# A selective-scan kernel: a quarter of the second half's products made a chunk ahead, norm and gate passes of the last direction in other places

## The chip, the cores and the metric

The kernel runs on one core of a Trainium2 chip. Its time is the device time of one execution in microseconds (us). The kernel before was run three times: 32539.59, 32542.47 and 32545.17 us, median 32542.47. The engines are PE (matmul; its weight loads are listed apart as PEld), DVE (vector), ACT (activation functions), POOL (general), and SP, which issues most of the DMAs. Each engine works through its own instructions in the order in which they were written, and semaphores tie the engines to one another.

## What is computed

The input is an image of 256 x 256 tokens with 128 channels. Layer 0 is a gated attention along the rows, layer 1 a selective scan in four directions; each is added to its input. The change lies in layer 1. Cut to what matters there:

```python
xz = x @ w_in.T;  xi, z = jnp.split(xz, 2, axis=-1);  z = silu(z)
xc = silu(depthwise_conv3x3(xi) + conv_b)              # 256 channels
xs = four orders of the tokens: rows, columns, and both backwards
dts, Bs, Cs = split(x_proj_w @ xs)                     # 8 + 16 + 16 rows
delta = softplus(dt_w @ dts + dt_bias)
# for each direction, channel and each of 16 states n, along the tokens t:
#   h[t] = exp(delta[t] * A[n]) * h[t-1] + (delta[t] * x[t]) * B[n, t]
#   y[t] = sum over n of h[t] * C[n, t]  + D * x[t]
y = sum of the four directions, each put back into row order
y = (y - mean) / sqrt(var + 1e-5) * ln_w + ln_b        # over the channels
out = x + (y * z) @ w_out.T
```

## The kernel before

**Stages.** The group norm, the attention and the convolution come first and take about 5.7 ms. The scan takes the rest; the change is in it alone.

**Directions and chunks.** The directions are worked one after the other, in the order 2, 1, 3, 0 (`ORDER`), each in 128 chunks of 512 tokens. The first three write their sum so far to DRAM (`store`); the next one loads it (`load_sum`, tile `yl`) and adds it on PE. The last direction (`finish`) adds all, normalizes over the channels, multiplies with the gate z, and projects to the output.

**Steps.** A chunk has eight steps, `g` = 0 to 7, called the first to the eighth step here. A step works on 32 channels with all 16 states on 128 partitions: four groups of 32 partitions, and for each group four states, one after the other along the free axis. So a step has four places, `n` = 0 to 3, each with one `exp` on ACT (`dA`, or `dAl` at n = 0; L1081) and one scan on DVE (L1107). Three of the four inputs of the scans are made by DVE in one multiplication for the next step (`times_B`, L838, which reads `ur`, spread over the partitions by PE). The fourth input, that of n = 0, is made by another way: ACT multiplies the transposed delta*x (`duT`) with the transposed B (`B_t`), 16 products of 128 x 128 for each half of the channels (`products`, tile `bt0` for steps one to four, `bt1` for steps five to eight, one buffer each; L797), and PE turns them back step by step (`turn_back`, tile `bl`, L809). After a step POOL saves the last column of h (L1126) and multiplies h with C (L1127). PE sums over the states for four steps together (`sums`, L853): for the steps five to eight at the second step of the next chunk, for the steps one to four at the end of the sixth and the start of the seventh.

**Work in pieces.** Everything that prepares the next chunks is written as generators, and at each place, between the exp and the scan, the loop takes a piece from each: one of `turning` (duT for the next chunk), one of every generator in `later` (`store`, `finish`), one of `preparing` (`prepare`, for the chunk after the next), and `counts[g][n]` pieces of `multiplying`, each of them one product on ACT. The order of the instructions on each engine follows from that by hand; there is no planner.

- `prepare(q + 2)` begins at n = 1 of the sixth step of chunk q and goes on into chunk q + 1. Its pieces that matter here: `pb` on PE at n = 0 of the eighth step, `bc` on ACT, which reads it, at n = 2 of the eighth (L710), `pv` on PE at n = 3, abs and relu at n = 1 and 2 of the first step of the next chunk, then exp, log(1+...) and so on, and `lg`, the Ln, at n = 0 of the third step (L758). [...] a table load stands before the Ln and another before the next exp.
- `products(q + 1, 0)` is put in line at n = 2 of the sixth step and has to be done when `turn_back` for the next chunk is written, at n = 3 of the eighth. `products(q, 1)` is put in line at n = 1 of the second step and has to be done at n = 3 of the fourth.
- `finish` begins at n = 0 of the fourth step of the next chunk. `until(a, b)` lets b - a places pass. Its 17th piece, at n = 0 of the eighth step, is the first of four `yn` passes (L952), which subtract the mean and divide; PE turns `yn` at n = 3 of the second step a chunk later, and the two `gz` passes (L971) scale with ln_w and ln_b. POOL then multiplies with z.
- PSUM tiles with the tag "mm" (`pb`, `pv`, `tpb`, `tpz`, `ysum`, `po` and others) share two buffers; the exps use three PSUM buffers (`dA`) and two in SBUF (`dAl`); `bx` has eight.

Of the kernel before, what the change touches and what calls it, by code (L numbers as in the profile page):

```python
# [66 lines left out]
def attention_and_scan_kernel(  # L67
# [611 lines left out]
    def until(now, then):  # L679

        for _ in range(then - now):
            yield
# [121 lines left out]
    def turn_back(q, g):  # L804

        bl = sps.tile([P, T], F32, name="bl", bufs=1)
        bt = products_of[q, g // 4]
        for b in range(4):
            nc.tensor.transpose(  # L809
                bl[:, b * P : (b + 1) * P], bt[:, b, g % 4].rearrange("t j c -> t (j c)"), ident  # L810
            )
        return bl
# [97 lines left out]
    def finish(q, yos):  # L910

        a = steps[q][1]
        yl = summed.pop(q)
        yield
        sums_ = []
        for g in range(2):
            ps = sps.tile([P, 2, DI], F32, name="ysum", tag="mm")
            add_sum(  # L920
                ps,
                yl[:, 2 * g : 2 * g + 2, :],
                [
                    (ps[:, j, h * P : (h + 1) * P], yos[h][:, (2 * g + j) * P : (2 * g + j + 1) * P])
                    for j in range(2)
                    for h in range(2)
                ],
            )
            sums_.append(ps)
            yield  # L930
        yield
        ys = io.tile([P, 4, DI], F32, name="ys", tag="yt", bufs=1)
        for g, ps in enumerate(sums_):
            nc.scalar.copy(ys[:, 2 * g : 2 * g + 2, :], ps)
            yield
        zt = io.tile([P, 2, T], F32, name="zl", bufs=1)
        nc.sync.dma_start(zt, z_d[:, a : a + T].rearrange("(h p) t -> p h t", p=P))
        st = io.tile([P, 4, 6], F32, name="yst")
        mv = io.tile([P, 4, 2], F32, name="ymv")
        rs = io.tile([P, 4], F32, name="yrs")  # L940
        nb = io.tile([P, 4], F32, name="ynb")
        for j in range(4):
            nc.vector.bn_stats(st[:, j, :], ys[:, j, :])
        for j in range(4):
            nc.vector.bn_aggr(mv[:, j, :], st[:, j, :])
        rsqrt(nc, rs, mv[:, :, 1], 1e-5, neg_half)
        nc.gpsimd.tensor_tensor(nb, mv[:, :, 0], rs, ALU.mult)
        nc.gpsimd.tensor_scalar(nb, nb, -1.0, None, ALU.mult)
        yield from until(6, 16)
        yn = io.tile([P, 4, DI], F32, name="yn", tag="yl", bufs=1)  # L950
        for j, now, then in ((0, 16, 19), (1, 19, 20), (2, 20, 23), (3, 23, 27)):
            nc.scalar.activation(  # L952
                yn[:, j, :],
                ys[:, j, :],
                AF.Identity,
                bias=nb[:, j : j + 1],
                scale=rs[:, j : j + 1],
            )
            yield from until(now, then)
        tps = []  # L960
        for h in range(2):
            tp = sps.tile([P, T], F32, name="tpz", tag="mm")
            for j in range(4):
                nc.tensor.transpose(
                    tp[:, j * P : (j + 1) * P], yn[:, j, h * P : (h + 1) * P], ident
                )
            tps.append(tp)
        yield from until(27, 30)
        gz = io.tile([P, 2, T], F32, name="gz", bufs=1)
        for h, tp in enumerate(tps):  # L970
            nc.scalar.activation(  # L971
                gz[:, h, :], tp, AF.Identity, bias=lnb_s[:, h : h + 1], scale=lnw_s[:, h : h + 1]
            )
            yield
        yield from until(32, 36)
        nc.gpsimd.tensor_tensor(gz, gz, zt, ALU.mult)
        yield from until(36, 40)
        xr = io.tile([P, 4, D], F32, name="xr", bufs=1)
        nc.sync.dma_start(xr, x2_d[a : a + T, :].rearrange("(j p) c -> p j c", p=P))
        yield from until(40, 55)  # L980
        po = sps.tile([P, 4, D], F32, name="po", tag="mm")
        nc.tensor.matmul(po, ident, xr, start=True, stop=True)
        for j in range(4):
            for h in range(2):
                nc.tensor.matmul(
                    po[:, j, :],
                    gz[:, h, j * P : (j + 1) * P],
                    wout_s[:, h, :],
                    start=False,
                    stop=True,  # L990
                    skip_group_check=True,
                )
        yield from until(55, 58)
        xo = io.tile([P, 4, D], F32, name="xo", tag="xr", bufs=1)
        nc.scalar.copy(xo, po)
        nc.sync.dma_start(out[a : a + T, :].rearrange("(j p) c -> p j c", p=P), xo)

    NQ = len(steps)
# [4 lines left out]
    def piece(*dues):  # L1003
        for due in dues:
            while due:
                try:
                    next(due[0])
                    return
                except StopIteration:
                    due.pop(0)  # L1010

    def drain(due):
        while due:
            piece(due)
# [42 lines left out]
    begin_sums(0, 0)  # L1057
    turning, multiplying, summing = [], [], []
    bls = {(0, 0): turn_back(0, 0)}

    counts = {1: [0, 2, 3, 3], 3: [2, 2, 2, 2], 5: [0, 0, 2, 2], 6: [1, 1, 2, 2], 7: [2, 2, 2, 0]}
    for s, (q, g) in enumerate(all_steps):
        k, a = steps[q]
        nxt = all_steps[s + 1] if s + 1 < len(all_steps) else None
        if g == 1:
            drs[q, 1] = spread_delta(q, 1)
        if g == 2 and q and steps[q - 1][0] != ORDER[0]:
            summed[q - 1] = load_sum(q - 1)
        if g == 2 and q + 2 < NQ:
            load(q + 2)  # L1070
        if g == 5 and q + 1 < NQ:
            drain(preparing)
            drs[q + 1, 0] = spread_delta(q + 1, 0)
        dr = drs[q, g // 4][:, g % 4, :]
        hs = bxs.pop((q, g))
        for n, i in enumerate((NB, *range(NB))):
            if i < NB:
                dA = sps.tile([P, T], F32, name="dA", bufs=3)
            else:
                dA = wk.tile([P, T], F32, name="dAl")  # L1080
            nc.scalar.activation(  # L1081
                dA, dr, AF.Exp, scale=A_s[:, k, g // 4, g % 4, i : i + 1]
            )
            if n == 0 and g == 3 and q:
                evacuate(q - 1, 1)
                begin_sums(q, 0)
            if n == 2 and g == 7:
                evacuate(q, 0)
                begin_sums(q, 1)
            if n == 0 and g == 1 and q:  # L1090
                drain([sums(q - 1, 1)])
            if n == 0 and g == 6:
                drain(summing)
            if g == 4 and n == 3 and q + 1 < NQ:
                turning.append(turn(q + 1))
            if g == 5 and n == 2 and q + 1 < NQ:
                multiplying.append(products(q + 1, 0))
            if g == 1 and n == 1:
                multiplying.append(products(q, 1))
            if g == 5 and n == 1 and q + 2 < NQ:  # L1100
                preparing.append(prepare(q + 2))
            piece(turning)
            pieces(later)
            piece(preparing)
            for _ in range(counts[g][n] if g in counts else 0):
                piece(multiplying)
            nc.vector.tensor_tensor_scan(  # L1107
                hs[:, i, :],
                dA,
                hs[:, i, :] if i < NB else bls.pop((q, g)),  # L1110
                0.0 if a == 0 else hst[:, g, i : i + 1],
                ALU.mult,
                ALU.add,
            )
            if n == 1 and nxt:
                bxs[nxt] = times_B(nxt[0], urs.pop(nxt))
            if n == 3 and nxt:
                bls[nxt] = turn_back(*nxt)
            if n == 3 and s + 2 < len(all_steps):
                urs[all_steps[s + 2]] = spread_du(*all_steps[s + 2])  # L1120
            if n == 3 and g == 5:
                summing.append(sums(q, 0))
                piece(summing)
        if g % 4 == 3:
            del drs[q, g // 4]
        nc.gpsimd.tensor_copy(hst[:, g, :], hs[:, :, T - 1])  # L1126
        nc.gpsimd.tensor_tensor(hs, hs, prepared[q][4], ALU.mult)  # L1127
        hcs[q, g] = hs
# [64 lines left out]
```

## Time and profile before

| | us | share of the span |
|---|---|---|
| median of three runs | 32542.47 | |
| profiled execution, its own time | 32538.74 | |
| its span, first to last instruction | 32537.0 | |
| PE busy | 24581.2 | 76% |
| DVE busy | 29634.3 | 91% |
| ACT busy | 25277.6 | 78% |
| POOL busy | 25719.5 | 79% |
| scans on DVE, n = 1 to 3 (L1107) | 15061.1 | x12192, 1262 ns each |
| times_B on DVE (L838) | 7067.5 | x4096, 1725 ns each |
| h * C on POOL (L1127) | 18604.5 | x4096, 4542 ns each |
| products on ACT (L797) | 5625.5 | x16384, 394 ns each |

The profile comes from one execution. Instructions on one engine can overlap by some tens of ns, so the spacing of their starts is shorter than their duration. In a timeline, a line gives the start in us from the first instruction, the duration, the engine, the line of the kernel, and in brackets how long the engine was idle before and what ended that. The clock that PE was granted is told as a share of its full speed.

### The profile page before, as it was taken

The numbers are of one execution on the slowest core, as the hardware profiler recorded it, in microseconds if no ns is written. First come the engines' busy times: TensorE is split into PE (matmuls) and PEld (weight loads), VectorE is DVE, ScalarE is ACT, GpSimd is POOL, SyncE is SP. The second block draws the span as 40 slices with busy tenths as digits, with TensorE's granted clock in tenths as the row PEclk, the third lists the DMA queues.
The fourth block names the chain that finished last, engine by engine and source line by source line (L and its number), as shares of the span: only waits on it lengthen the run. The fifth ranks groups of instructions, "written<-read, shape, count | busy, mean of one in ns | idle before, by whom it ended". The sixth has DMA issues, their size and how long they took to land.

```text
span 32537.0 us, 380541 instructions
## 1 busy us (share of the span) xinstructions
PE 24581.2 (76%) x122902; PEld 11561.7 (36%) x122902; DVE 29634.3 (91%) x28991; ACT 25277.6 (78%) x50438; POOL 25719.5 (79%) x11291
## 2 busy tenths in 40 slices
PE   5999989777777777777777777777777777777777
PEld 2555544223222223333333333333333333333333
DVE  7666643999999999999999999999999999999999
ACT  4555522888888888888888888888888888888887
POOL 3222200899999999999999999999999999999998
PEclk8999999777777777777777777777777777777777
DMA  3001023444444444444444444444444455554554
GB/s 137 29 28 30 28 93 123 110 108 109 110 109 108 108 109 119 118 118 119 120 120 118 117 119 121 119 119 118 120 120 118 118 123 123 122 121 121 122 122 112
DMA packets 2100469, 3518.55 MB, mean 108 GB/s; under 512 B 201112, under 2 KB 1187096, under 8 KB 2022560
## 3 DMA queue, kind: packets, MB, share of 16 engines
q1 hardware_dynamic: 2093296, 3476.09, 42.8%
q8 instruction: 967, 15.84, 0.2%
q10 hardware_dynamic: 5168, 18.12, 0.1%
q14 instruction: 1038, 8.50, 0.1%
HBM read 2754.18 MB, written 739.25 MB: 107 GB/s over the span
## 4 chain that ended last, share of the span: by engine, by line
DVE 31%; PE 27%; ACT 26%; issue 10%; POOL 5%; DMA 1%; DVEq 0%; SPq 0%; POOLq 0%; ACTq 0%
DVE bx L1107 17%; DVE bx L838 9%; PE yp L853 7%; ACT dA L1081 6%; PE ur L827 5%; ACT bt L797 4%; POOL bx L1127 2%; ACT dAl L1081 2%; PE pc L526 2%; ACT L758 2%; ACT L1081 2%; PE av L356 2%; POOL at L333 2%; ACT du L751 2%; PE atp L345 2%
## 5 line engine op out<-in xcount | busy, mean ns | idle before, releaser
L1127 POOL TENSOR_TENSOR bx<-bx,C_r 128x2048 f32<-128x2048 f32 x4096 | 18604.5, 4542 | 334.5 <-POOL hst L1126 6.0
L1107 DVE TENSOR_TENSOR_SCAN bx<-dA,hst,bx 128x512 f32<-128x512 f32 x12192 | 15061.1, 1262 | 455.3 <-ACT dA L1081 455.3
L1081 ACT ACTIVATE dA<-dr,A_s 128x512 f32<-128x512 f32 x12288 | 8345.5, 684 | 2974.6 <-DVE bx L1107 2865.2
L827 PE MATMUL ur<-du,spread 128*128 128x512 f32 x8192 | 5998.0, 823 | 4593.9 <-DVE bx L838 4544.3
L838 DVE TENSOR_TENSOR bx<-B_r,ur 128x1536 f32<-128x1536 f32 x4096 | 7067.5, 1725 | 39.1 <-DMA dr<-de_d 39.1
L797 ACT ACTIVATE bt<-duT,B_t 128x128 f32<-128x128 f32 x16384 | 5625.5, 394 | 0.0
L1107 DVE TENSOR_TENSOR_SCAN bx<-dAl,hst,bl 128x512 f32<-128x512 f32 x4064 | 5091.9, 1253 | 5.3 <-PE bl L809 4.3
L853 PE MATMUL yp<-bx,gather 128*32 128x512 f32 x32768 | 4808.1, 739 | 7.4 <-POOL bx L1127 6.4
L809 PE MATMUL bl<-ident,bt 128*128 128x128 f32 x16384 | 2817.3, 297 | 2060.9 <-DVE bx L1107 2049.9
L827 PEld LDWEIGHTS ur<-du,spread 128*128 128x128 f32 x8192 | 1519.7, 232 | 5194.1 <-DVE bx L838 5178.5
L809 PEld LDWEIGHTS bl<-ident,bt 128*128 128x128 f32 x16384 | 1871.7, 148 | 3949.2 <-DVE bx L1107 2874.1
L333 POOL TENSOR_TENSOR at<-at,sm 128x2048 f32<-128x2048 f32 x256 | 922.3, 3603 | 2708.9 <-DVE sm L332 2595.6
L1081 ACT ACTIVATE dAl<-dr,A_s 128x512 f32<-128x512 f32 x4096 | 2915.1, 712 | 0.0
L853 PEld LDWEIGHTS yp<-bx,gather 128*32 128x32 f32 x32768 | 1110.2, 134 | 4153.9 <-issue 4018.1
L1126 POOL COPY hst<-bx 128x4 f32<-128x4 f32 x4096 | 773.6, 189 | 1830.0 <-DVE bx L1107 1800.0
L325 ACT ACTIVATE at<-at,mx 128x256 f32<-128x256 f32 x2048 | 1016.1, 498 | 472.3 <-DVE mx L321 467.9
L755 POOL TENSOR_TENSOR e<-e,du 128x1024 f32<-128x1024 f32 x512 | 1206.6, 2357 | 137.7 <-DMA C_r<-bc_d 137.7
L766 POOL TENSOR_TENSOR du<-delta,xs 128x1024 f32<-128x1024 f32 x512 | 1208.9, 2361 | 40.2
L762 POOL TENSOR_TENSOR delta<-delta,lg 128x1024 f32<-128x1024 f32 x512 | 1208.8, 2361 | 40.2
L721 PE MATMUL pv<-bc,dtw_s 8*128 8x512 f32 x2048 | 1014.3, 614 | 256.8 <-ACT bc L710 256.8
L760 POOL TENSOR_TENSOR lg<-lg,e 128x1024 f32<-128x1024 f32 x512 | 1204.9, 2353 | 0.2 <-ACT lg L758 0.2
L354 DVE COPY aT<-atp 128x512 f32<-128x512 f32 x512 | 353.5, 690 | 772.8 <-PE atp L345 772.8
(172 smaller groups left out, 33209.5 us busy)
## 6 DMA issues: line engine op xcount, KB each, us to landing
dr<-de_d SPq DMA_DIRECT2D x4096, 256.0 KB
C_r<-bc_d SPq DMA_DIRECT2D x2048, 256.0 KB
B_r<-bc_d SPq DMA_DIRECT2D x2048, 192.0 KB
de_d<-delta SPq DMA_DIRECT2D x512, 512.0 KB
xtok<-xc_d SPq DMA_DIRECT2D x256, 512.0 KB
xtok<-xc_d SPq DMA_DIRECT2D x512, 256.0 KB
yl<-y_d SPq DMA_DIRECT2D x512, 256.0 KB
y_d<-yt SPq DMA_DIRECT2D x512, 256.0 KB
```

Source lines behind the costliest of these rows:

```text
L333: nc.gpsimd.tensor_tensor(at, at, sm.unsqueeze(3).to_broadcast([P, H, 2, S]), ALU.mult,)
L755: nc.gpsimd.tensor_tensor(e, e, du, ALU.subtract)
L762: nc.gpsimd.tensor_tensor(delta, delta, lg, ALU.add)
L766: nc.gpsimd.tensor_tensor(du, delta, xs, ALU.mult)
L797: nc.scalar.mul(bt[:, b, :, j, :], duT[:, b, h * P : (h + 1) * P].rearrange("t (g c) -> t g c", c=32), B_t[:, b, n : n + 1],)
L809: nc.tensor.transpose(bl[:, b * P : (b + 1) * P], bt[:, b, g % 4].rearrange("t j c -> t (j c)"), ident)
L827: nc.tensor.matmul(ur, spread[:, g % 4].rearrange("p j c -> p (j c)"), prepared[q][2][:, g // 4, :], start=True, stop=True,)
L838: nc.vector.tensor_tensor(bx[:, :NB, :], prepared[q][3], ur.unsqueeze(1).to_broadcast([P, NB, T]), ALU.mult,)
L853: nc.tensor.matmul(yp[32 * g : 32 * g + 32, :], gather, hc[:, i, :], start=(i == 0 and steps[q][0] != ORDER[0]), stop=True, skip_group_che ...
L1081: nc.scalar.activation(dA, dr, AF.Exp, scale=A_s[:, k, g // 4, g % 4, i : i + 1])
L1107: nc.vector.tensor_tensor_scan(hs[:, i, :], dA, hs[:, i, :] if i < NB else bls.pop((q, g)), 0.0 if a == 0 else hst[:, g, i : i + 1], ALU.mult,
L1127: nc.gpsimd.tensor_tensor(hs, hs, prepared[q][4], ALU.mult)
```

## The change

It has two parts. In `products` for the second half, four of the 16 pieces of the next chunk are now taken in the eighth step, at n = 1 and n = 2, so the generator is put in line there and not in the second step of its own chunk. The counts of all steps are set anew: the second step has 4 instead of 8, the sixth 6 instead of 4, the seventh 8 instead of 6. For the first chunk the four pieces are made before the loop. In `finish`, which runs in the last direction only, the four `yn` passes move from the 17th, 20th, 21st and 24th piece to the 16th, 17th, 20th and 21st, and the two `gz` passes from the 31st and 32nd to the 32nd and 33rd. What is computed stays the same.

```diff
-        yield from until(6, 16)
+        yield from until(6, 15)
         yn = io.tile([P, 4, DI], F32, name="yn", tag="yl", bufs=1)
-        for j, now, then in ((0, 16, 19), (1, 19, 20), (2, 20, 23), (3, 23, 27)):
+        for j, now, then in ((0, 15, 16), (1, 16, 19), (2, 19, 20), (3, 20, 27)):
             nc.scalar.activation(
                 yn[:, j, :],
                 ys[:, j, :],
...
             tps.append(tp)
-        yield from until(27, 30)
+        yield from until(27, 31)
         gz = io.tile([P, 2, T], F32, name="gz", bufs=1)
         for h, tp in enumerate(tps):
             nc.scalar.activation(
                 gz[:, h, :], tp, AF.Identity, bias=lnb_s[:, h : h + 1], scale=lnw_s[:, h : h + 1]
             )
             yield
-        yield from until(32, 36)
+        yield from until(33, 36)
         nc.gpsimd.tensor_tensor(gz, gz, zt, ALU.mult)
...
     begin_sums(0, 0)
     turning, multiplying, summing = [], [], []
     bls = {(0, 0): turn_back(0, 0)}
-
-    counts = {1: [0, 2, 3, 3], 3: [2, 2, 2, 2], 5: [0, 0, 2, 2], 6: [1, 1, 2, 2], 7: [2, 2, 2, 0]}
+    multiplying.append(products(0, 1))
+    for _ in range(4):
+        piece(multiplying)
+
+
+    counts = {1: [0, 0, 2, 2], 3: [2, 2, 2, 2], 5: [0, 0, 3, 3], 6: [2, 2, 2, 2], 7: [2, 2, 2, 0]}
...
             if g == 5 and n == 2 and q + 1 < NQ:
                 multiplying.append(products(q + 1, 0))
-            if g == 1 and n == 1:
-                multiplying.append(products(q, 1))
+            if g == 7 and n == 1 and q + 1 < NQ:
+                multiplying.append(products(q + 1, 1))
```

## The prediction

> **What bounds it now.** I read the page first: over the span DVE is busy longest.
>
> ```profile
> PE 24581.2 (76%) x122902; PEld 11561.7 (36%) x122902; DVE 29634.3 (91%) x28991; ACT 25277.6 (78%) x50438; POOL 25719.5 (79%) x11291
> ```
>
> The scan phase runs from 5714 to 32486 us. There the question is only when DVE stands still, so next the waits of DVE, once for the first three directions (6000 to 25500 us) and once for the last (25600 to 32470 us): total, times, longest.
>
> ```profile
> DVE bx L1107 <- ACT dA L1081: 205.9, 378, 1.6
> DVE bx L1107 <- ACT dA L1081: 248.1, 125, 2.2
> ```
>
> That is one wait per chunk (128 chunks a direction) and nearly nothing else. The timeline of ACT and the scan that waits, in one chunk of the last direction (chunk start 28557.52), shows where:
>
> ```profile
> 28564.35 0.71 ACT L797 ACTIVATE bt<-duT,B_t 128x128 f32<-128x128 f32 x2
> 28564.95 0.69 ACT L1081 ACTIVATE dA<-dr,A_s 128x512 f32<-128x512 f32 x1
> 28565.56 0.60 ACT L995 COPY xo<-po 128x512 f32<-128x512 f32 x1
> 28566.04 1.00 ACT L797 ACTIVATE bt<-duT,B_t 128x128 f32<-128x128 f32 x3
> 28566.92 0.70 ACT L1081 ACTIVATE dA<-dr,A_s 128x512 f32<-128x512 f32 x1
> ...
> 28569.17 1.28 ACT L758 ACT_TABLE_LOAD   x1
> 28570.46 1.06 ACT L758 ACTIVATE lg<-lg 128x1024 f32<-128x1024 f32 x1
> 28571.53 1.28 ACT L1081 ACT_TABLE_LOAD   x1
> 28572.83 1.30 ACT L1081 ACTIVATE dA<-dr,A_s 128x512 f32<-128x512 f32 x2
> 28573.56 1.28 DVE L1107 TENSOR_TENSOR_SCAN bx<-dA,hst,bx 128x512 f32<-128x512 f32 x1 [1.99 <-ACT dA L1081]
> ```
>
> Two table loads and the Ln lie between two exps of the third step (g = 2). ACT reaches them with too little lead, and the scan waits 1.99 us, in a steady chunk of the first three directions 0.38. The products (bt) just ahead of them are what the change moves.
>
> How much lead ACT has is decided earlier, at the copy bc in the eighth step: ACT waits there for PE, and from there to the Ln it works without a pause. So I compared two chunks of the second direction; PE's granted clock is the first number after POOL:
>
> ```profile
> 12653.36:12656.77 3.41, 2.98 (x10) 0.82 (x14) 3.41 (x4) 1.80 (x5) 3.41 (x1) 0.50 0.00 0
> 12656.78:12667.01 10.23, 9.46 (x51) 3.11 (x44) 10.23 (x9) 9.06 (x20) 9.52 (x5) 1.00 0.04 13
> 12704.56:12711.38 6.82, 6.22 (x22) 1.50 (x26) 6.82 (x6) 5.05 (x12) 6.74 (x3) 0.50 0.00 0
> 12711.39:12725.03 13.64, 10.08 (x46) 3.70 (x38) 13.64 (x12) 10.85 (x20) 11.35 (x5) 1.00 0.28 63
> ...
> 12663.22 0.58 ACT L710 COPY bc<-pb 40x512 f32<-40x512 f32 x1 [0.69 <-PE pb L704]
> 12716.20 0.58 ACT L710 COPY bc<-pb 40x512 f32<-40x512 f32 x1 [2.30 <-PE pb L704]
> 12683.10 1.28 DVE L1107 TENSOR_TENSOR_SCAN bx<-dA,hst,bx 128x512 f32<-128x512 f32 x1 [0.38 <-ACT dA L1081]
> 12735.66 1.28 DVE L1107 TENSOR_TENSOR_SCAN bx<-dA,hst,bx 128x512 f32<-128x512 f32 x1 [1.57 <-ACT dA L1081]
> ```
>
> The first scan of the seventh step (g = 6) starts at 12656.03 and 12707.40. In the first chunk the clock rises 0.75 us after it, in the second 3.99; bc comes 0.34 us before the second scan of the eighth step (12663.56), and 1.27 after it (12714.93). The next chunk's stall grows from 0.38 to 1.57. Call the rise T and the place of bc b. Read over all chunks, b is -0.34 at T = 0.75, -0.11 from 1.2 to 2.0, +0.61 at 2.65, +1.30 at 4.03: a rise 1 us later costs half of it, because PE goes at half speed until then.
>
> [...] every change lies on a grid of 3.413 us. So a chunk has a phase against this grid. [...]
>
> **The change part by part**, for the profiled execution: 32538.7 us, 32537.0 of span and 1.7 around it, 3.7 under the median of 32542.5.
>
> (1) Four products leave the second step (g = 1): two at n = 1, one each at n = 2 and 3. By starts above: 28564.95 - 28564.35 = 0.60 for two, 0.88/3 = 0.29 for each other: 1.18 us less ACT work ahead of the Ln.
>
> (2) They are made in the eighth step instead (n = 1, 2), whose count stays 2, 2, 2: the first half's products go earlier, +1 at g = 5 n = 2, 3 and g = 6 n = 0, 1: 4 x 0.29 = 1.2 us. The cover is ACT's idle time there, 1.83 us ahead of one exp of the seventh step (28598.36), more in the sixth. Nothing; without the cover 1.2 us less lead, which gives (1) back.
>
> (3) The new wait: the first product of the eighth step overwrites the half that PE's last turn_back (bl, g = 7) reads. Queued behind it on ACT: another product, two more, exp, yo, bc. In the steady chunk this product would start 0.56 us before bl ends, in the chunk with the late clock 1.94 (12711.52 against 12713.46). But PE still has ur and pb to do after bl, 2.7 us, and ACT needs only two products, exp and yo, 1.7 us, before it waits for pb anyway: the wait comes out of bc's idle time of 0.7 to 2.3 us. Price 0, bounds 0 and 0.3 us a chunk.
>
> (4) Last direction only: the passes yn move from n = 0, 3 of the eighth and 0, 3 of the first step to n = 3 of the seventh, 0 and 3 of the eighth, 0 of the first. Past bc there are now two, not three: 28608.92 - 28608.43 = 0.49 us less. One more lies ahead of bc, whose idle time in this direction is 0.82: it fits. Together 1.67 us less ahead of the Ln.
>
> (5) The gz passes move one place, past the Ln: 2 x 0.66 us either way; the second now follows the yo copy, and PE's ysum, which needs its PSUM buffer, comes later (behind two ur of the next times_B). Nothing. No DMA, PE, POOL or DVE instruction moves, and no queue of SP or POOL is passed. Four products of chunk 0 before the loop: 1.2 us once.
>
> If that were all, the stall would fall from 0.38 to 0 and from 1.99 to 0.32: rival B. But the stall is what holds the chunk to the clock's grid.
>
> **The period.** Without stalls a step takes 1.172 + 2.820 + 1.194 + 1.175 = 6.361 us between scan starts, a chunk 50.89. In three directions a stalled chunk takes 50.89 + 0.48 = 51.37; where b exceeds 0.08, 0.38 + b replaces 0.46. Fifteen windows are 51.20, so T falls 0.17 a chunk; below 0.7 it jumps a window up, to about 4, two late chunks follow, and it starts again near 2: some ten chunks averaging 51.54. The trace has 6596, 6598 and 6598 us for 128, or 51.53 to 51.55. The last direction has 54.82 + b, which at b = -0.21, T = 1.01 is 54.61, exactly sixteen windows; it sits there in nearly every chunk.
>
> After, first three: 50.89 + max(0, 0.38 + b - 1.18). With no stall T rises 0.31 a chunk, until b = 1.11 (T = 3.66, below the jump at 4.1) brings a stall of 0.31: 51.20, fifteen windows, and this holds, since a later T adds stall. It needs (1) to be worth 0.8 to 1.4. So 19792 - 384 x 51.20 = 131 us gained.
>
> After, last: 54.82 + b - 1.67 = 53.15 + b. Sixteen windows would need b = 1.46; the largest b seen is 1.33. So T climbs through about 0.8, 2.6, 3.5, 3.9, 4.1 and jumps: 52.8, 53.7, 54.2, 54.4, sometimes 54.5: mean 53.8 to 53.9 against 54.61; 0.76 x 125 = 95 us. Sum 226: 32538.7 - 226 = 32313, and 32316 in the shown runs.
>
> **Covers that shrink.** POOL idles 4.6 us a chunk (3.8 in the last direction); it lags DVE by up to 5.7 us after the third step and is level again by the eighth. The load yl lands about 17.5 us into the chunk, by the DMA packets, some 1.8 us before PE uses it (2.9 in the last direction); DVE comes to it 0.2 to 0.8 us earlier. PE then still has 0.5 to 1.1 us in hand (1.8 in the last). Nothing; without that cover up to 0.3 us a chunk.
>
> **Rivals.** A, as above: 0.50; 32270 to 32350. B, the stalls simply vanish, no phase: three directions 232, the last 211, 32096, shown 32100: 0.10. For it: the sum of edits; against: b and T go together in every chunk before. C, the last direction keeps sixteen windows (enough that its saving is 1.55 and not 1.67, or the jump lies 0.1 higher): only 131, 32411: 0.16. D, the three directions don't hold at fifteen windows but near 51.0, or the last finds 53.5: another 50 to 110, about 32230: 0.13. E, slower: the wait of (3) isn't covered. It decides once bc comes more than 1.2 us later than now; at 2 us, 0.8 x 384 + 0.3 x 128 = 350 us, 32890. Against: the 1 us between 2.7 and 1.7. 0.07. No change, a new stall at bl in the fifth step eating it: 0.04. That the products fail to move can't be: the counts add to sixteen each.
>
> A measurement tells from no change what exceeds about 0.2%, 65 us. Faster is A to D, 0.89; same 0.04; slower 0.07. The range 32190 to 32425 holds A, C and most of D, about 0.78.
>
> **What would show it.** DVE's wait on dA: about 0.2 to 0.3 us in nearly every chunk of the first three directions, spread between 0.2 and 1.9 in the last; chunk starts 51.20 apart; T near 3.66 there; bc late by 1.1. B would show almost none. Waits of bt on bl of 0.5 to 2 us with bc no later than T says: (3) right. Wrong if DVE waits appear at bl or ur, or if the clock no longer decides bc.

## The result, and the profile after

The changed kernel takes 32312.33 us, the median of 32309.63, 32309.72, 32314.95 and 32316.99. Its ratio to the kernel before is 0.9929, with a 95% interval of 0.9912 to 0.9946: about 231 us faster (with a fourth run, of 32546.18 us, the median of the kernel before is 32543.82). The profiled execution took 32314.95 us, with a span of 32313.2. The page shows how busy the engines were:

```profile
PE 23871.2 (74%) x122902; PEld 10880.6 (34%) x122902; DVE 29629.7 (92%) x28991; ACT 25191.1 (78%) x50438; POOL 25710.2 (80%) x11291
```

The work is the same as before: the same numbers of instructions, and DVE, ACT and POOL busy for the same time within 90 us. PE does the same work in 710 us less; its mean granted clock over the span is 0.851, where it was 0.818. The waits of DVE, for the first three directions and then for the last:

```profile
DVE bx L1111 <- ACT dA L1085: 66.8, 324, 0.7
DVE bx L1111 <- PE bl L809: 10.9, 11, 1.9
...
DVE bx L1111 <- ACT dA L1085: 147.8, 124, 1.9
DVE bx L1111 <- PE bl L809: 13.8, 39, 1.1
```

The wait for dA has shrunk from 205.9 to 66.8 us and from 248.1 to 147.8, but it has not gone: it comes 324 times in the first three directions and 124 times in the last, still about once a chunk. New are waits for bl, the tile that PE turns back, 24.7 us in the two views together. ACT's waits over the whole scan phase, after and then before, show what the moved products meet:

```profile
ACT bt L797 <- PE bl L809: 706.7, 483, 1.9
ACT bc L710 <- PE pb L704: 450.7, 510, 0.9
...
ACT bc L710 <- PE pb L704: 521.3, 510, 2.4
```

The products wait for bl in nearly every chunk, as forecast, and bc still waits for pb behind them. Nothing on ACT went past such a wait: its 42880 instructions of the scan start, in both traces, in the order in which the kernel writes them. The four directions, as stretches of the trace, cut where DVE starts its first scan of each (the last to the last scan):

```profile
5715.60:12268.00 6552.40, 4567.76 (x19414) 1790.84 (x19414) 6525.03 (x5120) 5549.65 (x10753) 5995.51 (x2558) 0.83 0.46 109
12268.00:18818.60 6550.60, 4665.89 (x20470) 1925.94 (x20470) 6524.03 (x5121) 5556.51 (x10754) 6000.56 (x2560) 0.83 0.49 120
18818.60:25372.80 6554.20, 4661.44 (x20484) 1922.76 (x20484) 6524.88 (x5121) 5556.28 (x10753) 6000.61 (x2560) 0.83 0.49 120
25372.80:32261.90 6889.10, 5058.89 (x23687) 2428.72 (x23686) 6726.01 (x6136) 5977.91 (x11593) 6492.17 (x3190) 0.82 0.51 123
```

Divided by 128 the first three give 51.19, 51.18 and 51.20 us a chunk. The starts of the first scan in consecutive chunks lie 51.20 us apart in the median (51.195 to 51.200 in the three directions): fifteen windows of 3.413 us. A window is the step of the grid on which PE's granted clock changes: the clock records of this trace have it at 0.5 or 1.0, and its 3168 changes lie within 0.002 us of a grid of 3.41333 us, as do the 3674 in the trace of the kernel before. At 0.5 the transposes of bl start 0.214 us apart in the median, at 1.0 0.110. The last direction has 53.85 us a chunk, by the starts of its chunks. The gain is made up as forecast: 6596 + 6598 + 6598 - 6552 - 6551 - 6554 = 135 us in three directions where 131 were forecast, 6980 - 6889 = 91 in the last where 95 were.

The next view gives the granted clock (the first number after POOL) in stretches that begin where the clock rises: two consecutive chunks of the second direction, then three of the last.

```profile
15993.10:16000.00 6.90, 6.23 (x29) 1.98 (x22) 6.90 (x7) 4.27 (x11) 6.43 (x3) 1.00 0.04 10
16044.30:16051.00 6.70, 6.03 (x29) 1.88 (x22) 6.70 (x6) 4.07 (x10) 6.48 (x3) 1.00 0.04 9
28427.86:28438.09 10.23, 9.46 (x51) 3.15 (x44) 10.23 (x9) 9.93 (x23) 10.07 (x5) 1.00 0.61 120
28482.47:28490.00 7.53, 6.86 (x37) 2.10 (x27) 7.53 (x6) 6.41 (x16) 7.37 (x5) 1.00 0.66 129
28537.08:28545.00 7.92, 7.25 (x33) 2.27 (x26) 7.92 (x7) 6.35 (x16) 7.84 (x3) 1.00 0.39 72
```

In the second direction the rises are 51.20 us apart, and the first scan of the seventh step starts at 15989.51 and 16040.71, so T, the rise after that scan, is 3.59 both times. In the last direction that scan starts at 28427.14, 28479.94 and 28533.65: T is 0.72, 2.53 and 3.43, and climbs from chunk to chunk. The timeline of the same chunks, ACT in the eighth step (of the second direction first), then the scan of the third step in the next chunk:

```profile
15995.42 0.69 ACT L797 ACTIVATE bt<-duT,B_t 128x128 f32<-128x128 f32 x2 [1.72 <-PE bl L809]
15996.01 0.67 ACT L1085 ACTIVATE dA<-dr,A_s 128x512 f32<-128x512 f32 x1
15996.63 0.58 ACT L1026 COPY yo<-yp 128x512 f32<-128x512 f32 x1
15998.12 0.58 ACT L710 COPY bc<-pb 40x512 f32<-40x512 f32 x1 [0.91 <-PE pb L704]
16016.41 1.28 DVE L1111 TENSOR_TENSOR_SCAN bx<-dA,hst,bx 128x512 f32<-128x512 f32 x1 [0.20 <-ACT dA L1085]
...
28434.32 0.58 ACT L710 COPY bc<-pb 40x512 f32<-40x512 f32 x1 [0.30 <-PE pb L704]
28454.08 1.28 DVE L1111 TENSOR_TENSOR_SCAN bx<-dA,hst,bx 128x512 f32<-128x512 f32 x1 [0.25 <-ACT dA L1085]
28488.02 0.58 ACT L710 COPY bc<-pb 40x512 f32<-40x512 f32 x1 [0.91 <-PE pb L704]
28507.78 1.28 DVE L1111 TENSOR_TENSOR_SCAN bx<-dA,hst,bx 128x512 f32<-128x512 f32 x1 [1.15 <-ACT dA L1085]
28542.18 0.58 ACT L710 COPY bc<-pb 40x512 f32<-40x512 f32 x1 [0.91 <-PE pb L704]
28561.94 1.28 DVE L1111 TENSOR_TENSOR_SCAN bx<-dA,hst,bx 128x512 f32<-128x512 f32 x1 [1.59 <-ACT dA L1085]
```

Two things are to be seen. First, the new wait: the product in the eighth step waits 1.72 us for bl, and still bc waits another 0.91 us for pb behind it. Second, in the last direction bc starts 0.35 us before the second scan of the eighth step, then 0.55 and 0.99 us after it (those scans start at 28434.67, 28487.47 and 28541.19); this place of bc is the b of the prediction. The stall that follows is 0.25, 1.15 and 1.59 us: between these chunks it rises with b, one for one. The exception is the 19 chunks that follow T near 4.13, b near 1.34. There the scans already wait for bl in the first and the second step, 0.24 and 0.43 us, and the stall for dA is 1.05.

### The profile page after: what moved, and what is told of

The parts are those of the page before. It is cut to its first block, busy times and chain, and to the rows that moved or that the text cites. A ratio compares the mean times of both kernels' runs of the same rounds, so it can differ in the third digit from the quotient of the medians.

```text
span 32313.2 us, 380670 instructions
## 1 busy us (share of the span) xinstructions
PE 23871.2 (74%) x122902; PEld 10880.6 (34%) x122902; DVE 29629.7 (92%) x28991; ACT 25191.1 (78%) x50438; POOL 25710.2 (80%) x11291
## 4 chain that ended last, share of the span: by engine, by line
PE 31%; ACT 23%; DVE 21%; issue 12%; POOL 11%; DMA 2%; SPq 0%; ACTq 0%; POOLq 0%; DVEq 0%
DVE bx L1111 10%; PE yp L853 7%; DVE bx L838 7%; POOL bx L1131 7%; ACT dA L1085 6%; PE ur L827 5%; ACT bt L797 2%; PE pb L704 2%; PE pc L526 2%; PE av L356 2%; ACT dAl L1085 2%; PE tpy L876 2%; POOL at L333 2%; ACT e L728 2%; PE atp L345 2%
## 5 line engine op out<-in xcount | busy, mean ns | idle before, releaser
L827 PE MATMUL ur<-du,spread 128*128 128x512 f32 x8192 | 5712.8, 787 | 4498.4 <-DVE bx L838 4375.3
L853 PE MATMUL yp<-bx,gather 128*32 128x512 f32 x32768 | 5049.5, 770 | 7.9 <-POOL bx L1131 6.4
L809 PE MATMUL bl<-ident,bt 128*128 128x128 f32 x16384 | 2717.1, 290 | 2445.1 <-DVE bx L1111 2442.7
L809 PEld LDWEIGHTS bl<-ident,bt 128*128 128x128 f32 x16384 | 1791.2, 143 | 4330.0 <-DVE bx L1111 3249.6
L827 PEld LDWEIGHTS ur<-du,spread 128*128 128x128 f32 x8192 | 1452.6, 223 | 5027.5 <-DVE bx L838 5024.1
```

The source lines that it names most:

```text
L809: nc.tensor.transpose(bl[:, b * P : (b + 1) * P], bt[:, b, g % 4].rearrange("t j c -> t (j c)"), ident)
L827: nc.tensor.matmul(ur, spread[:, g % 4].rearrange("p j c -> p (j c)"), prepared[q][2][:, g // 4, :], start=True, stop=True,)
L853: nc.tensor.matmul(yp[32 * g : 32 * g + 32, :], gather, hc[:, i, :], start=(i == 0 and steps[q][0] != ORDER[0]), stop=True, skip_group_che ...
```

## The experiments

Two theories were put against each other. The grid theory is that of the prediction: the stall in the third step depends on when PE's clock rises, the clock changes only on the grid of 3.413 us seen in the traces of both kernels, and a chunk settles at a whole number of windows where it can. The queue theory counts work alone: each us of ACT work taken from ahead of the Ln is a us less stall, until the stall is gone. T, b and the time of a chunk are read from the trace of each run: T and b as the median over the chunks of a direction, the time of a chunk as the mean where no median is named. Four kernels were run to tell these apart, three to take the clock's effect away, and two to find what comes next. Times with one run behind them are one execution; the kernel before took 32544.92 us beside the first four, and 32548.21 and 32547.62 as medians beside the others.

### The products alone

```diff
 (the changed kernel, with the finish function of the kernel before)
-        yield from until(6, 15)
+        yield from until(6, 16)
...
-        for j, now, then in ((0, 15, 16), (1, 16, 19), (2, 19, 20), (3, 20, 27)):
+        for j, now, then in ((0, 16, 19), (1, 19, 20), (2, 20, 23), (3, 23, 27)):
...
-        yield from until(27, 31)
+        yield from until(27, 30)
...
-        yield from until(33, 36)
+        yield from until(32, 36)
```

> The products part alone; the yn and gz passes stay where they were before. Grid theory (the clock's 3.413 us windows hold the chunk): the first three directions at 51.20 us a chunk as in the changed kernel; the last has 54.82 + b - 1.18, which reaches sixteen windows, 54.61, at b = 0.97, T = 3.4, and sits there: nothing gained in the last direction, about 32408 us. Queue theory (each us taken from ACT ahead of the Ln is a us less stall): the last direction 0.49 us a chunk longer than in the changed kernel, about 32374 us.

Measured: 32403.44 us. The last direction, as one stretch:

```profile
25371.30:32350.20 6978.90, 5097.89 (x23690) 2492.74 (x23690) 6722.02 (x6136) 5990.44 (x11593) 6495.42 (x3190) 0.81 0.50 121
```

That is 6978.9 us against 6980 before: 1.18 us of ACT work less in each of its chunks, and nothing gained. The median chunk takes 54.614 us, T is 3.35 to 3.38 and b 0.96 in nearly all of them. b was -0.21 before: bc now comes 1.17 us later, which takes up the 1.18 us. The first three directions are as in the changed kernel, 51.20.

### The yn and gz passes alone

```diff
 (the kernel before, with the finish function of the changed kernel)
-        yield from until(6, 16)
+        yield from until(6, 15)
...
-        for j, now, then in ((0, 16, 19), (1, 19, 20), (2, 20, 23), (3, 23, 27)):
+        for j, now, then in ((0, 15, 16), (1, 16, 19), (2, 19, 20), (3, 20, 27)):
...
-        yield from until(27, 30)
+        yield from until(27, 31)
...
-        yield from until(32, 36)
+        yield from until(33, 36)
```

> The yn and gz passes alone; the products as before. Grid theory: 0.49 us of ACT work less in the last direction gains nothing, since T moves to the jump of b near 2.5 and goes to and fro around it at a mean of 54.61: about 32543 us, the same as before. Queue theory: 125 x 0.49 = 61 us faster, about 32482 us.

Measured: 32544.01 us beside 32544.92. No gain, as the grid theory has it. The waits of DVE in the last direction were 248.1 us before, and are not less now:

```profile
DVE bx L1107 <- ACT dA L1081: 258.0, 125, 2.8
```

One detail of the expectation was wrong: T doesn't go to and fro around 2.5, it sits at 2.00 with b = 0.28, which is 0.49 later than before and takes up the 0.49 us. In the last direction b has no flat stretch between 1.2 and 2.5, which had been read from the other three; it follows one line, T/2 - 0.71, through all the points seen (-0.21 at 1.01, 0.28 at 2.00, 0.55 at 2.53, 1.23 at 3.9). The two passes, yn and gz, were not run apart from each other.

So neither part gains anything in the last direction, and both together gain 91 us there.

### Three products ahead in place of four

```diff
-    for _ in range(4):
+    for _ in range(3):
         piece(multiplying)
...
-    counts = {1: [0, 0, 2, 2], 3: [2, 2, 2, 2], 5: [0, 0, 3, 3], 6: [2, 2, 2, 2], 7: [2, 2, 2, 0]}
+    counts = {1: [0, 1, 2, 2], 3: [2, 2, 2, 2], 5: [0, 0, 3, 3], 6: [2, 2, 2, 2], 7: [2, 1, 2, 0]}
```

> The change with three products ahead in place of four (one less at n = 1 of the eighth step, one more at n = 1 of the second). Grid theory: the first three directions still at exactly 51.20 us, T now near 3.0 and b near 0.8 where they were 3.6 and 1.08, the stall unchanged near 0.2; the last at 54.61 with T near 3.8; about 32408 us. Queue theory: 0.29 us more stall in every chunk, the first three at 51.49, the last at 54.1, about 32462 us.

Measured: 32406.47 us. The second direction and the last as stretches, the clock of one chunk of the second direction, then bc in that chunk and the scan that waits in the next:

```profile
12271.00:18821.40 6550.40, 4738.34 (x20473) 1996.80 (x20472) 6525.07 (x5121) 5559.74 (x10753) 6000.96 (x2560) 0.80 0.49 120
25375.50:32352.70 6977.20, 5133.53 (x23686) 2470.26 (x23686) 6722.28 (x6135) 5978.38 (x11593) 6492.34 (x3190) 0.81 0.50 121
15995.52:16002.00 6.48, 5.81 (x32) 1.74 (x25) 6.48 (x6) 3.84 (x11) 6.02 (x3) 1.00 0.00 0
...
16000.83 0.58 ACT L710 COPY bc<-pb 40x512 f32<-40x512 f32 x1 [1.21 <-PE pb L704]
16019.40 1.28 DVE L1111 TENSOR_TENSOR_SCAN bx<-dA,hst,bx 128x512 f32<-128x512 f32 x1 [0.20 <-ACT dA L1085]
```

A product put back ahead of the Ln should lengthen the stall by 0.29 us. It doesn't: 6550.4 us against 6550.6, and the same stall of 0.20. What gives way is the phase: T is 3.01 in place of 3.59, half of the 0.58 is what b falls, from 1.08 to 0.79, and that is the 0.29. The last direction locks at 54.61 again, at T = 3.77.

### Six products ahead

```diff
-    for _ in range(4):
+    for _ in range(6):
         piece(multiplying)
...
-    counts = {1: [0, 0, 2, 2], 3: [2, 2, 2, 2], 5: [0, 0, 3, 3], 6: [2, 2, 2, 2], 7: [2, 2, 2, 0]}
+    counts = {1: [0, 0, 1, 1], 3: [2, 2, 2, 2], 5: [0, 0, 3, 3], 6: [2, 2, 2, 2], 7: [2, 4, 2, 0]}
```

> The change with six products ahead (four at n = 1 of the eighth step, two at n = 2; one each at n = 2 and 3 of the second). 1.77 us less ahead of the Ln in the first three directions, 2.26 in the last. Grid theory: the largest b, 1.34, no longer causes a stall there, nothing holds the chunk at fifteen windows, T sweeps over its whole range, 50.89 us a chunk; the last near 52.9: about 32070 us. Queue theory: stalls of 0.29 and 0.59 us less than in the changed kernel: about 32120 us. Either is slower by what the four products at n = 1, behind the wait for bl, may delay bc.

Measured: 32146.59 us, slower than either theory said, so that the total doesn't tell them apart. The trace does; the waits of DVE from 6000 to 25000 us:

```profile
DVE bx L1111 <- PE bl L809: 24.8, 28, 1.6
DVE bx L1111 <- ACT delta L729: 1.2, 5, 0.2
DVE bx L1111 <- ACT yt L903: 0.5, 1, 0.5
```

The stall for dA is gone. In the first direction a chunk takes 50.88 us, and T sweeps from 0.75 to 4.12: the lock is gone too. The second and third have 50.97 and 51.03, because in 11 and 20 chunks the scan at the start of the fifth step waits up to 1.6 us for bl. The last has 53.23 in place of 52.9. Two things are new there: ACT's idle time before bc is gone in four chunks of ten, because four products stand behind the wait for bl; and bl is late in the fifth step, 0.13 us a chunk. The last run below, which loads yl earlier and for that writes yn in another place, keeps the first and takes the second away, and has 52.88. That puts the excess down to the fifth step.

### PE kept busy: the clock's effect taken away

```diff
             tp = sps.tile([P, T], F32, name="tps", tag="mm")
-            for j in range(4):
+            for j in 3 * [0, 1, 2, 3]:
                 nc.tensor.transpose(
...
         bt = products_of[q, g // 4]
-        for b in range(4):
+        for b in (5 if g in (5, 6) else 1) * [0, 1, 2, 3]:
             nc.tensor.transpose(
```

In the changed kernel:

> The changed kernel with idle time of PE filled: bl of the sixth and seventh step is turned back five times over, the transposes of xtok three times over, the last result counts. Nothing else changes. Grid theory: PE is then at full clock when the sums begin, b stays near -0.34 in every chunk, no stall in the first three directions (50.89 us a chunk), 52.8 in the last: about 32070 us, 240 faster than the changed kernel although PE does more work. [...] Queue theory without the grid: more PE work on the way to bc gives nothing or costs, 32312 us or more.

In the kernel before:

> The kernel before with the same filling of PE. Grid theory: the late chunks go, 51.37 us a chunk in the first three directions (0.17 less than 51.54), 54.48 in the last (0.13 less): about 32460 us; and the difference to the changed kernel with the filling is what the change is worth without the grid: 384 x 0.48 + 127 x 1.67 = 396 us. Queue theory: 32544 us or more, and a difference as between the two kernels, 231 us.

Measured: 32139.12 us on the changed kernel (ratio to before 0.9874, 0.9859 to 0.9888), and 32459.21 us on the kernel before. PE has 24576 matmuls more to do, and the kernels are 173 and 89 us faster. The first and the last direction of the changed kernel with the filling:

```profile
5719.00:12232.60 6513.60, 5019.90 (x25562) 2473.77 (x25562) 6511.57 (x5120) 5568.98 (x10754) 6005.49 (x2558) 0.88 0.46 110
25290.90:32083.80 6792.90, 5509.55 (x29803) 3045.98 (x29802) 6728.11 (x6135) 5973.78 (x11592) 6496.52 (x3190) 0.90 0.52 125
```

The mean clock is 0.88 and 0.90 where it was 0.83 and 0.82. At the start of the seventh step PE has the full clock in 511 of the 512 chunks; in the changed kernel it has it in none. b is -0.40 in nearly every chunk of the last direction, the first direction runs at DVE's own 50.89 us a chunk, and of the last direction's stall for dA 0.19 us are left of 1.16. On the kernel before, the median chunk takes 51.37 and 54.42 us, and no late chunks are left. With the filling in both, the change is worth 320 us; the 396 expected, and the 32070 us, are not reached. Most of the 76 us that are missing are waits for bl in the fifth step, 68 us in all: 0.3 us a chunk in the last direction and 0.1 in the second and third. The waits of DVE over the scan phase of the changed kernel with the filling (the longest, 11.6 us, stands at its start):

```profile
DVE bx L1111 <- PE bl L809: 79.3, 88, 11.6
DVE bx L1111 <- ACT dA L1085: 26.7, 125, 2.0
```

### Filling and six products together, and yl loaded earlier

> Six products ahead and the filling together. Grid theory: the first three directions at 50.89 with at most a few waits in the fifth step, the last near the DVE's own 52.5: about 32035 us, the fastest of all. Queue theory: as six ahead alone, 32147 us, or more.

Measured: 32136.88 us (0.9873, 0.9857 to 0.9889): 102 us above the expectation, no better than with four, and nearer to the queue theory's figure. No stall for dA is left in the last direction, but the scans wait 0.62 us a chunk for bl in the fifth step. The waits of PE in the last direction suggest a cause:

```profile
PE ysum L876 <- DMA yl<-y_d: 94.0, 79, 3.0
```

So the load was moved:

```diff
-        if g == 2 and q and steps[q - 1][0] != ORDER[0]:
+        if g == 0 and q and steps[q - 1][0] != ORDER[0]:
             summed[q - 1] = load_sum(q - 1)
...
-        yn = io.tile([P, 4, DI], F32, name="yn", tag="yl", bufs=1)
+        yn = ys
```

> Six products ahead, the filling of PE, and the load of yl issued at the first step in place of the third; for that the yn passes write over ys, so that the last direction does not wait for yn to free yl's buffer. If the waits of the scans for bl in the fifth step come from yl landing late (PE's ysum waits for it): they go, about 0.1 us a chunk in the second and third direction and 0.7 in the last: 50.89 and 52.5 us a chunk, about 32015 us. If something else on PE is late: no change against 32137 us.

> The same without the filling of PE. Grid theory: the first three directions at 50.89, the last still thrown about by the clock at about 53.1: about 32090 us. Queue theory without the grid: the same as with the filling, or less.

Measured: 32015.71 us with the filling (ratio 0.9837, 0.9821 to 0.9854), 32070.53 without it. With it the trace has no wait of DVE left between 5750 and 31960 us; a chunk takes 50.87 to 50.89 us in the first three directions and 52.44 in the last. Without it the first three are as fast, and the last, at 52.88, still has waits for dA of 0.4 us on average in the third step. So the late yl was the cause of the waits in the fifth step, and once they are gone the filling is worth another 55 us, where the queue theory had nothing or a loss. The kernel with all of it is the fastest, 297 us under the changed one and 532 under the one before.

## Why the prediction was right

The time was 4 us under the forecast, and the steps that led there hold one by one. That it came so close is in part luck: the gain was 4 us larger than forecast in the first three directions and 4 us smaller in the last.

- **What bounds it.** The one stall for dA in each chunk, ahead of which ACT works without a pause from bc on. Right: from bc to the Ln no gap of ACT is over 0.02 us in 508 of the 512 chunks, where before the longest was 0.08 us in the median; DVE's wait for dA fell from 454.0 us in the two views before to 214.6, and no other wait of DVE in them came to more than the 24.7 us for bl.
- **Products and yn passes.** 1.18 and 0.49 us were right as sizes. From one seventh step to the next, a chunk with b above 0.1 takes 51.29 + b before and 50.12 + b after in the first three directions, 1.17 less; in the last 54.82 + b and 53.16 + b, 1.66 less against the 1.67 of the two together. The parts alone give 1.17 and 0.49 in the last direction, as b moved. With the filling, which takes the clock out, the last direction went from 54.42 to 52.78 in the median chunk, 1.65.
- **The new wait at nothing.** The products waited 707 us in all for bl, up to 1.9 us at once, and bc kept 0.30 us of idle time or more behind it in every chunk; b at a given T did not grow (0.63 at T = 2.69 in the first three directions, before and after). The 0.56 us that the prediction gives for the product's lead over bl in the steady chunk holds for T from 1.2 to 2.1; in the steady chunk it shows, at T = 0.75, it is 0.34, and the price stays the same. Taking the wait away, with a second buffer, was not tried. With six products and the filling, bc's idle time is gone in the last direction and b is -0.16 in place of -0.40; even there no stall for dA follows.
- **The lock at fifteen windows.** T = 3.66 and b = 1.11 were forecast, 3.60 and 1.08 came. The small difference is the prediction's own sum: it takes 50.89 + 0.38 + b for a late chunk before, 51.27 + b, where the trace has 51.29 + b. That it is a lock and not a sum that happens to give 51.20 is shown by the run with three products, which kept 51.20 and moved T, and by the filling, which ended it.
- **The last direction.** 0.8, 2.6, 3.5, 3.9, 4.1 were forecast for T; 0.8, 2.55, 3.45, 3.9 and 4.13 are where nearly all chunks lie. From the seventh step at each of these T to the next seventh step it is 52.85, 53.73, 54.17, 54.39 and 54.51 us, against 52.8, 53.7, 54.2, 54.4 and 54.5; the mean is 53.85, between the 53.8 and 53.9 named. The forecast of sixteen windows being just out of reach was the tightest step: 1.38 us less work, with three products and the passes, in place of 1.67 locks it.
- **Rivals.** B, the sum without a phase, was 212 us too low for this kernel. With the clock held up by the filling the time comes within 39 us of it. C, the last direction held at sixteen windows, is what the products alone give: 32403.44 us against its 32411. D and E didn't come.
- **A sign of being wrong that came.** The prediction named waits of DVE for bl as one. They came, 24.7 us in the two views above, too small to change the sum. In the last direction 12.7 of the 13.8 us lie in the first and second step, after T near 4.13; this the prediction didn't name. In the second and third they lie in the fifth step, in 12 chunks, and in 10 of these PE had waited for yl: the cover named as shrinking. It was enough for this change but was the next bound, as the later runs show. The price given for losing it, up to 0.3 us a chunk, was too low: with six products and the filling it was 0.6 in the last direction.

One reading was too wide: the flat stretch of b between T = 1.2 and 2.0 holds in the first three directions and not in the last. The forecast for the last direction didn't use that stretch. In the run with six products the stretch goes on to T = 2.5 in the first three directions, and b jumps there from -0.04 to 0.55; what makes it flat, and why it ends so, stays open.

## What to carry to other kernels

When a loop's period is an exact multiple of a fixed interval, as here of the 3.413 us on whose grid the clock of PE changed in the traces, look for what ties it there before adding up savings. Here a stall that grew when the loop got ahead and shrank when it fell behind took up small savings whole: in the last direction 0.49, 1.18 and 1.38 us a chunk gained nothing, and 1.67 gained 0.76. The test is cheap: put a little work back and see whether the time or only the phase moves. And an engine off the critical path can be worth more work: repeated transposes on a partly idle PE made this kernel 173 us faster.

## What the runs showed of the hardware that was not expected

- Repeated transposes raised the clock that PE was granted: with bl and tps repeated it is 0.88 and 0.90 on average in the first and last direction in place of 0.83 and 0.82. Each transpose is a weight load and a matmul in the trace (16384 of each for bl in the changed kernel); their effects were not tried apart.
- A scan whose initial value is a constant and not a column of a tile took less: 1202 ns against 1262 in the kernel before, for the scans of n = 1 to 3. The first chunk of a direction, 32 such scans, is 1.9 us shorter where nothing stalls, 48.95 us against 50.89 in the second and third direction of the run with six products.
